# Four states in one exponential, a VectorE sum and a four-stream epilogue in the last layer of a selective-scan network

## The chip, the cores and the metric

The kernel runs on one core of one Trainium2 chip. The core has five engines with queues of their own[...]: TensorE (matmuls into PSUM), VectorE, ScalarE (activations), GpSimd (POOL in the profile) and SyncE (SP), which issues the DMA transfers. The metric is the device time of one execution in microseconds: the median of three runs.

## The reference

Four layers follow each other on x of shape (8, 48, 48, 96). Each adds to x a two-dimensional selective scan of its group-normalised input:

```
xz = gn(x) @ in_proj ;  xc, z = split(xz)            # 192 channels each
u  = silu(depthwise_conv3x3(xc) + conv_b)
for each of 4 directions k (rows, columns, and both reversed):
    dts, B, C = x_proj_k(u)                            # B and C: 16 states
    delta = softplus(dt_proj_k(dts) + bias)
    layers 0-2:  h = h * exp(delta*A) + (delta*u)*B ;  y = sum_n h*C
    layer 3:     decay = exp(cumsum(delta*A))
                 h = decay * cumsum(delta*B*u / (decay + 1e-12)) ;  y = sum_n h*C
y = sum of the directions + u * D
x = x + (layernorm(y) * silu(z)) @ out_proj
```

Layer 3 has no recurrence: its decay is a running product over the whole sequence, so with growing position exp(A * cumsum(delta)) falls until it is zero in float32, and what is added there is zero too.

## The kernel before

The eight images are taken as four pairs. For each pair the 2 x 192 channels are three tiles of 128 partitions (tile 0 and 1: the first 128 channels of each image; tile 2: the remaining 64 of both). Two phases (rows, columns) times two directions times three tiles make 12 groups for each layer and pair.

In layers 0 to 2 a group is three chunks of 768 positions with 16 states each, class `Chunk`; these units fill the first 19.6 ms. Their order within the engines is written out by hand: `keep_order` ties every instruction to the one before it on its engine. The last layer runs in a short form, class `Edge`: of each group only the 192 positions (`EDGE`) at the start of the scan are computed. The kernel checks at the end that the decay is exactly zero beyond them (`faded`, line 827) and would run the long form if it were not (lines 1199 to 1206); it doesn't here. For the short form there is no written order; the framework's scheduler orders the instructions of each engine by their place in the program and by its own estimate of when they are ready, gives out buffers, and sets all the waits.

A unit of the short form is four states (`QUAD`), handled as one tile of 128 x (4 x 192); four units make a group, and 4 x 12 x 4 = 192 units the layer. The steps of a unit, with their lines:

- `load` (857): DMA brings the four rows of C, spread over the partitions, into a "cb" tile.
- `decay` (864): ScalarE computes exp(A_n * dl) for the four states, one activation of 192 elements each, since A_n is a value per partition, passed as the activation's scale. dl is the running sum of delta (line 823), made by VectorE once for each group. The result is a "da" tile, of which there are five.
- `spread` (871, 872, 877): ScalarE makes rq = exp(-ln(da + 1e-12)), a "bb" tile of three; TensorE spreads four rows of B over the partitions into PSUM, a "b" tile of two.
- `scan` (882, 883, 885, 889, 890): VectorE multiplies b by delta*u and by rq and takes four running sums of 192; GpSimd multiplies C by da and the product by the running sums.
- `add_up` (897): TensorE adds the four products into one PSUM bank, as matmuls with the identity. At the group's end `collect` (919) adds that bank to y on VectorE.

The loop in `run` (1148 to 1184) takes one unit at a time. `get_ready` issues the decay three units ahead of the scan, and `add_up` comes four units (`LAG`) after it. Each group has a preparation (`prepare`, lines 573 to 607), which computes delta and delta*u through TensorE, ScalarE, GpSimd and VectorE, and then calls `sum_up` (823). After every unit ten steps of side work are issued (`side_step`): the epilogue of the pair before and the prologue of the pair after, whose 3 x 3 convolution is line 301.

The epilogue (926 to 1053) is a generator that goes through 16 chunks (`ECHUNKS`) of 144 positions. A chunk loads x and y (956, 958), subtracts the mean over channels by matmuls (940 to 946), squares (981), takes the mean of the squares by matmuls again, makes the scale by Ln and Exp (990, 991), multiplies (993), applies gain and offset (996), computes z by matmuls (1002, 1006), its silu (259, with a table load before and, at line 260, one after), multiplies (1015) and projects (1041 to 1043), copies (1047) and stores (1049). Its PSUM banks come from a pool of two (`bank`); its loads go one chunk ahead. The last pair's epilogue has no units beside it: line 1191 runs it to its end by itself.

Of the kernel before, what the change touches and what calls it, by code (L numbers as in the profile page):

```python
# [39 lines left out]
F32 = mybir.dt.float32  # L40
BF16 = mybir.dt.bfloat16
AF = mybir.ActivationFunctionType
ALU = mybir.AluOpType
# [6 lines left out]
P = 128  # L50
NB, H, W, DM = 8, 48, 48, 96
L = H * W
DIN = 192
NS = 16
# [8 lines left out]
EDGE = 4 * W  # L63
QUAD = 4
# [5 lines left out]
BANK = 512  # L70

SCAN = 16 * W
# [3 lines left out]
ECHUNKS = [(r * W, min(EROWS, H - r) * W) for r in range(0, H, EROWS)]  # L76
# [26 lines left out]
def ss2d_layers_kernel(ctx: ExitStack, tc: tile.TileContext, x_in, consts, weights, out):  # L103
    nc = tc.nc
# [25 lines left out]
    ident = cst[:, 0:P]  # L130
# [131 lines left out]
    def bank():  # L262
        return psum.tile([P, BANK], F32, name="ps", tag="ps")
# [353 lines left out]
    def columns_of(l, t, ph, d, n):  # L617
        k = ph + 2 * d
        return layers[l].a[:, int(t == 2), k * NS + n : k * NS + n + 1]
# [189 lines left out]
    class Edge:  # L809
# [51 lines left out]
        def decay(self, i):  # L861
            self.da[i] = da = self.quad(apool.tile([P, SCAN], F32, name="da", tag="da"))
            for j in range(QUAD):
                nc.scalar.activation(  # L864
                    da[:, j, :], self.dl, AF.Exp,
                    scale=columns_of(self.l, self.t, self.ph, self.d, QUAD * i + j),
                )

# [23 lines left out]
        def add_up(self, i):  # L892
            if i == 0:
                self.acc = pacc.tile([P, 2 * BANK], F32, name="acc", tag="acc")
            c = self.cb.pop(i)
            for j in range(QUAD):
                nc.tensor.matmul(  # L897
                    self.acc[:, :EDGE], ident, c[:, j, :],
                    start=(i == j == 0), stop=(QUAD * i + j == NS - 1),
                )  # L900
            if QUAD * i + QUAD == NS:
                late_sums.append(self.collect)
# [22 lines left out]

    def epilogue(l, p):
        ly, s = layers[l], state[l, p]
# [7 lines left out]
        def over_channels(ps, z, own, own_2, tiles):  # L935


            for t in tiles:
# [4 lines left out]
                for b in range(2):  # L943
                    o = ps[half(b), 2, :]
                    nc.tensor.matmul(o, off[:, 0:64], z[:, b, :], start=True, stop=False)  # L945
                    nc.tensor.matmul(o, own_2[:, half(b)], z[:, 2, :], start=False, stop=True)

        def three():
            return bank()[:, : 3 * EM].rearrange("p (t m) -> p t m", t=3)

        loaded = {}

        def load(i):
            at = slice(ECHUNKS[i][0], sum(ECHUNKS[i]))
            x = sm2.tile([DM, 2, EM], F32, name="ex", tag="ex")
            nc.sync.dma_start(x, src[:, :, at].rearrange("b c m -> c b m"))
            y = sm2.tile([P, 3, EM], F32, name="ey", tag="ey")
            nc.sync.dma_start(y, yd[:, :, at].rearrange("t p m -> p t m"))
            loaded[i] = x, y

        load(0)
        for _ in range(3):
            yield
        for i, (c0, m) in enumerate(ECHUNKS):
            at = slice(c0, c0 + m)
            x, y = loaded.pop(i)

# [3 lines left out]
            over_channels(ps, y, centre, centre_22, (2,))  # L971
            xn = sm1.tile([DM, 2, EM], F32, name="exn", tag="exn")
            for b in range(2):
# [4 lines left out]
            yield True  # L978
            yc = sm1.tile([P, 3, EM], F32, name="eyc", tag="eyc")
            nc.scalar.copy(yc, ps)  # L980
# [24 lines left out]
            for b in range(2):  # L1005
# [3 lines left out]
                )  # L1009
            if i + 1 < len(ECHUNKS):  # L1010
                load(i + 1)
            yield True
# [22 lines left out]
            q = m // 2  # L1035
            ps = bank()[:q, : 4 * DM].rearrange("q (h b c) -> q h b c", h=2, b=2)
            for h in range(2):
# [14 lines left out]
            yield  # L1052
        del state[l, p]


    def drain(g):
        for _ in g:
            pass
# [38 lines left out]
    def run(pairs, short):  # L1097
# [92 lines left out]
        collected()  # L1190
        drain(epilogue(*pairs[-1]))

# [109 lines left out]
```

## Time and profile before

| | us |
|---|---:|
| median of 3 runs | 21633.64 (21624.16 to 21662.88) |
| the profiled execution's own time | 21617.61 |
| its span | 21615.8 |
| layers 0 to 2, up to the first short decay (line 864) | 19594 |
| short units of the last layer, up to the last addition to y (line 919) | about 1785 |
| last epilogue to the end of the span | 237 |

| busy, share of the span | TensorE | VectorE | ScalarE | GpSimd |
|---|---:|---:|---:|---:|
| whole span | 87% | 87% | 63% | 83% |

A group of instructions in the profile is a line such as "L897 PE MATMUL acc<-cb,cst 128*128 128x192 f32 x1536 | busy us, mean ns of one | idle time of the engine just before them, and what ended it". A float32 matmul leaves two records, so the 768 matmuls of line 897 count as 1536. The "chain" follows the work back from its end: at each step to what released it, or to the instruction before it on its engine.

### The profile page before, as it was taken

The numbers are of one execution on the slowest core, as the hardware profiler recorded it, in microseconds if no ns is written. First come the engines' busy times: TensorE is split into PE (matmuls) and PEld (weight loads), VectorE is DVE, ScalarE is ACT, GpSimd is POOL, SyncE is SP. The second block draws the span as 40 slices with busy tenths as digits, with TensorE's granted clock in tenths as the row PEclk, the third lists the DMA queues.
The fourth block names the chain that finished last, engine by engine and source line by source line (L and its number), as shares of the span: only waits on it lengthen the run. The fifth ranks groups of instructions, "written<-read, shape, count | busy, mean of one in ns | idle before, by whom it ended". The sixth has DMA issues, their size and how long they took to land. (4 is left out here: it accounts for less than half of the span.)

```text
span 21615.8 us, 229908 instructions
## 1 busy us (share of the span) xinstructions
PE 18860.1 (87%) x64898; PEld 9267.7 (43%) x64898; DVE 18857.4 (87%) x15938; ACT 13615.2 (63%) x24054; POOL 18001.9 (83%) x11081
## 2 busy tenths in 40 slices
PE   8888988988988988988988988988988988988786
PEld 3333443443443444444444444444444444444555
DVE  5999999999999999999999999999999999996443
ACT  4555665665665666665666666656656655666776
POOL 5988889889898898898898888888888888895442
PEclk9999999999999999999999999999999999998887
DMA  3666666666676676676676666666666566663221
GB/s 125 187 191 190 189 193 192 188 193 190 189 200 190 189 198 189 189 199 186 189 198 190 189 194 188 187 191 190 187 191 189 187 192 186 189 191 105 74 68 52
DMA packets 1707635, 3833.01 MB, mean 177 GB/s; under 512 B 238448, under 2 KB 575216, under 8 KB 1693168
## 3 DMA queue, kind: packets, MB, share of 16 engines
q1 hardware_dynamic: 1706352, 3818.21, 60.6%
q8 instruction: 523, 8.57, 0.2%
q14 instruction: 760, 6.23, 0.1%
HBM read 3665.08 MB, written 152.27 MB: 177 GB/s over the span
## 5 line engine op out<-in xcount | busy, mean ns | idle before, releaser
L788 PE MATMUL acc<-cb,cst 128*128 128x384 f32 x27648 | 10802.0, 520 | 0.0
L754 POOL TENSOR_TENSOR cb<-cb,da 128x768 f32<-128x768 f32 x5184 | 9362.0, 1816 | 1706.4 <-DVE da L745 1047.4
L788 PEld LDWEIGHTS acc<-cb,cst 128*128 128x128 f32 x27648 | 5045.4, 197 | 3982.6 <-issue 1503.7
L745 DVE TENSOR_TENSOR_SCAN da<-da,carry,b 128x768 f32<-128x768 f32 x3456 | 6267.1, 1813 | 219.3 <-DVE b L741 1.8
L741 DVE TENSOR_TENSOR b<-du,b 128x768 f32<-128x768 f32 x5184 | 4915.6, 948 | 966.9 <-PE b L729 960.2
L712 ACT ACTIVATE da<-dl,a 128x768 f32<-128x768 f32 x5184 | 4767.5, 926 | 90.5 <-POOL cb L754 57.9
L729 PE MATMUL b<-brow,pick 48*128 48x512 bf16 (+3 forms) x10368 | 2661.3, 338 | 1629.0 <-DVE da L745 1319.0
L712 ACT ACTIVATE b<-dl,a 128x768 f32<-128x768 f32 x1728 | 1559.8, 903 | 2956.9 <-DVE da L745 2841.7
L754 POOL TENSOR_TENSOR cb<-cb,bb 128x768 f32<-128x768 f32 x1728 | 3137.3, 1816 | 230.4 <-issue 61.6
L684 POOL TENSOR_TENSOR bb<-bb,du 128x768 f32<-128x768 f32 x1728 | 3136.8, 1815 | 131.5 <-DMA bb<-xd 105.3
L745 DVE TENSOR_TENSOR_SCAN da<-da,b 128x768 f32<-128x768 f32 x1728 | 3029.9, 1753 | 109.6 <-ACT b L712 1.9
L729 PEld LDWEIGHTS <-pick 48*128 48x128 bf16 (+1 forms) x10368 | 672.9, 97 | 4467.5 <-DVE da L745 2342.7
L745 DVE TENSOR_TENSOR_SCAN bb<-b,carry,bb 128x768 f32<-128x768 f32 x1152 | 2069.5, 1796 | 21.8 <-ACT b L712 15.2
L301 PE MATMUL ps<-pad,diag 128*128 128x480 f32 (+1 forms) x4320 | 1972.1, 557 | 7.5 <-ACT u L309 5.0
L638 ACT COPY carry<-da 128x1 f32<-128x1 f32 x3456 | 627.1, 181 | 1041.1 <-DVE da L745 1026.0
L578 ACT ACTIVATE ps<-ps,w 128x384 f32<-128x384 f32 (+1 forms) x912 | 497.2, 545 | 1113.0 <-PE ps L573 1111.1
L782 PE MATMUL acc<-y,cst 128*128 128x384 f32 x1296 | 807.3, 755 | 368.0 <-ACT y L803 194.8
L301 PEld LDWEIGHTS ps<-pad,diag 128*128 128x128 f32 x4320 | 800.0, 190 | 723.9 <-issue 310.8
L591 POOL TENSOR_TENSOR lg<-lg,w 128x384 f32<-128x384 f32 (+1 forms) x912 | 894.0, 980 | 224.7 <-ACT w L589 224.7
L745 DVE TENSOR_TENSOR_SCAN bb<-b,bb 128x768 f32<-128x768 f32 x576 | 999.6, 1735 | 34.1 <-ACT b L712 28.5
L592 POOL TENSOR_TENSOR lg<-lg,e 128x384 f32<-128x384 f32 (+1 forms) x912 | 890.5, 976 | 71.2
L573 PE MATMUL ps<-dts,w 6*128 6x384 f32 (+5 forms) x2432 | 814.7, 519 | 149.3 <-DVE du L599 63.9
(141 smaller groups left out, 17513.5 us busy)
## 6 DMA issues: line engine op xcount, KB each, us to landing
cb<-xd SPq DMA_DIRECT2D x4736, 384.0 KB
cb<-xd SPq DMA_DIRECT2D x4736, 192.0 KB
bb<-xd SPq DMA_DIRECT2D x1152, 384.0 KB
bb<-xd SPq DMA_DIRECT2D x1152, 192.0 KB
yd<-y SPq DMA_DIRECT2D x48, 1152.0 KB
ey<-yd SPq DMA_DIRECT2D x256, 216.0 KB
brow<-xb SPq DMA_DIRECT2D x576, 72.0 KB
ex<-xs SPq DMA_DIRECT2D x256, 108.0 KB
```

Source lines behind the costliest of these rows:

```text
L301: nc.tensor.matmul(ps[:, :m], ly.diag[:, int(t == 2), j, :], pad[:, r0 + dy : r0 + dy + nr, dx : dx + W], start=(j == 0), stop=(j == 8),)
L573: nc.tensor.matmul(o[:, :m], ly.dtw[q0 : q0 + r, k, chans], dts[q0 : q0 + r, at], start=True, stop=True,)
L591: nc.gpsimd.tensor_sub(lg, lg, w1)
L592: nc.gpsimd.tensor_add(lg, lg, e)
L684: nc.gpsimd.tensor_mul(b, b, self.du)
L712: nc.scalar.activation(da, self.dl, AF.Exp, scale=columns_of(self.l, self.t, self.ph, self.d, n))
L729: nc.tensor.matmul(b[:, z : z + zm], w, self.brow[:k, z : z + zm], start=True, stop=True)
L741: nc.vector.tensor_mul(b, self.du, b)
L745: nc.vector.tensor_tensor_scan(way(h), way(da), way(b), start, ALU.mult, ALU.add)
L754: nc.gpsimd.tensor_mul(c, c, h)
L782: nc.tensor.matmul(self.acc[:, a, : self.m // 2], w, self.y_part(z)[:, a], start=True, stop=False,)
L788: nc.tensor.matmul(self.acc[:, a, : self.m // 2], ident, c[:, a, :], start=False, stop=(n == NS - 1),)
```

## The change

In `Edge.decay` the four scaled exponentials become one product and one exponential: GpSimd multiplies dl, read four times, with the four columns of A, each read 192 times, into the da tile, and ScalarE takes one Exp of the 768 elements in place.

In `Edge.add_up` VectorE sums the four products over the state (a `tensor_reduce` that reads the tile with the state innermost), into the first 192 columns of a further "da" tile, and one identity matmul adds that sum to the PSUM bank.

The epilogue takes a part and a number of parts. The last pair's epilogue is run as four generators, each of which takes every fourth chunk; they are stepped in turn. Streams 0 and 1 share the pool of two banks, streams 2 and 3 use the two "b" tiles of PSUM. Streams 1 to 3 keep their tiles in one "tmp" tile each and load a chunk when they begin it; stream 0 keeps the old tiles and loads its next chunk ahead. Epilogues of other pairs keep one part.

```diff
--- before.py
+++ after.py
@@ -860,11 +860,15 @@
 
         def decay(self, i):
             self.da[i] = da = self.quad(apool.tile([P, SCAN], F32, name="da", tag="da"))
-            for j in range(QUAD):
-                nc.scalar.activation(
-                    da[:, j, :], self.dl, AF.Exp,
-                    scale=columns_of(self.l, self.t, self.ph, self.d, QUAD * i + j),
-                )
+            at = (self.ph + 2 * self.d) * NS + QUAD * i
+            nc.gpsimd.tensor_mul(
+                da,
+                self.dl.unsqueeze(1).to_broadcast([P, QUAD, EDGE]),
+                layers[self.l].a[:, int(self.t == 2), at : at + QUAD].unsqueeze(2).to_broadcast(
+                    [P, QUAD, EDGE]
+                ),
+            )
+            nc.scalar.activation(da, da, AF.Exp)
 
         def spread(self, i):
             self.rq[i] = rq = self.quad(bbpool.tile([P, SCAN], F32, name="rq", tag="bb"))
@@ -892,12 +896,14 @@
         def add_up(self, i):
             if i == 0:
                 self.acc = pacc.tile([P, 2 * BANK], F32, name="acc", tag="acc")
-            c = self.cb.pop(i)
-            for j in range(QUAD):
-                nc.tensor.matmul(
-                    self.acc[:, :EDGE], ident, c[:, j, :],
-                    start=(i == j == 0), stop=(QUAD * i + j == NS - 1),
-                )
+
+            c, total = self.cb.pop(i), apool.tile([P, SCAN], F32, name="da", tag="da")[:, :EDGE]
+            nc.vector.tensor_reduce(
+                total, c.rearrange("p n m -> p m n"), mybir.AxisListType.X, ALU.add
+            )
+            nc.tensor.matmul(
+                self.acc[:, :EDGE], ident, total, start=(i == 0), stop=(QUAD * i + QUAD == NS)
+            )
             if QUAD * i + QUAD == NS:
                 late_sums.append(self.collect)
 
@@ -923,7 +929,8 @@
                 nc.sync.dma_start(s["yd"][t], y)
 
 
-    def epilogue(l, p):
+    def epilogue(l, p, part=0, parts=1):
+
         ly, s = layers[l], state[l, p]
         gn, yd, src = s["gn"], s["yd"], x_store(l, p)
         dst = x_store(l + 1, p) if l + 1 < NLAYER else None
@@ -945,38 +952,59 @@
                     nc.tensor.matmul(o, off[:, 0:64], z[:, b, :], start=True, stop=False)
                     nc.tensor.matmul(o, own_2[:, half(b)], z[:, 2, :], start=False, stop=True)
 
+        def own_bank():
+            return bank() if part < 2 else pb.tile([P, 2 * BANK], F32, name="b", tag="b")
+
         def three():
-            return bank()[:, : 3 * EM].rearrange("p (t m) -> p t m", t=3)
+            return own_bank()[:, : 3 * EM].rearrange("p (t m) -> p t m", t=3)
 
         loaded = {}
 
         def load(i):
             at = slice(ECHUNKS[i][0], sum(ECHUNKS[i]))
-            x = sm2.tile([DM, 2, EM], F32, name="ex", tag="ex")
+            if part:
+                w = tmp.tile([P, 10 * EM], F32, name="ew", tag="tmp")
+                x, xn = (
+                    w[:DM, a * EM : a * EM + 2 * EM].rearrange("p (b m) -> p b m", b=2)
+                    for a in (0, 2)
+                )
+                y, yc = (
+                    w[:, a * EM : a * EM + 3 * EM].rearrange("p (t m) -> p t m", t=3)
+                    for a in (4, 7)
+                )
+            else:
+                x = sm2.tile([DM, 2, EM], F32, name="ex", tag="ex")
+                y = sm2.tile([P, 3, EM], F32, name="ey", tag="ey")
+                xn = yc = None
             nc.sync.dma_start(x, src[:, :, at].rearrange("b c m -> c b m"))
-            y = sm2.tile([P, 3, EM], F32, name="ey", tag="ey")
             nc.sync.dma_start(y, yd[:, :, at].rearrange("t p m -> p t m"))
-            loaded[i] = x, y
-
-        load(0)
+            loaded[i] = x, y, xn, yc
+
+        mine_of = range(part, len(ECHUNKS), parts)
+        load(part)
         for _ in range(3):
             yield
-        for i, (c0, m) in enumerate(ECHUNKS):
+        for i in mine_of:
+            c0, m = ECHUNKS[i]
             at = slice(c0, c0 + m)
-            x, y = loaded.pop(i)
+            if i not in loaded:
+                load(i)
+            x, y, xn, yc = loaded.pop(i)
 
             ps = three()
             over_channels(ps, y, centre, centre_22, (0, 1))
             yield True
             over_channels(ps, y, centre, centre_22, (2,))
-            xn = sm1.tile([DM, 2, EM], F32, name="exn", tag="exn")
+            if xn is None:
+                xn = sm1.tile([DM, 2, EM], F32, name="exn", tag="exn")
             for b in range(2):
                 nc.scalar.activation(
                     xn[:, b, :], x[:, b, :], AF.Identity,
                     bias=gn[:, b, 1:2], scale=gn[:, b, 0:1],
                 )
             yield True
-            yc = sm1.tile([P, 3, EM], F32, name="eyc", tag="eyc")
+            if yc is None:
+                yc = sm1.tile([P, 3, EM], F32, name="eyc", tag="eyc")
             nc.scalar.copy(yc, ps)
             nc.scalar.activation(y, ps, AF.Square)
             yield
@@ -1007,8 +1035,8 @@
                     ps[half(b), 2, :], ly.inw[:, DIN + P : 2 * DIN], xn[:, b, :],
                     start=True, stop=True,
                 )
-            if i + 1 < len(ECHUNKS):
-                load(i + 1)
+            if not part and i + parts < len(ECHUNKS):
+                load(i + parts)
             yield True
             silu(ps, ps)
             yield True
@@ -1033,7 +1061,7 @@
                 continue
 
             q = m // 2
-            ps = bank()[:q, : 4 * DM].rearrange("q (h b c) -> q h b c", h=2, b=2)
+            ps = own_bank()[:q, : 4 * DM].rearrange("q (h b c) -> q h b c", h=2, b=2)
             for h in range(2):
                 z = slice(h * q, h * q + q)
                 for b in range(2):
@@ -1050,7 +1078,9 @@
                     out[2 * p + b, at, :].rearrange("(h q) c -> q h c", h=2), st[:, :, b, :]
                 )
             yield
-        del state[l, p]
+        state[l, p]["left"] = state[l, p].get("left", parts) - 1
+        if not state[l, p]["left"]:
+            del state[l, p]
 
 
     def drain(g):
@@ -1188,7 +1218,9 @@
             c.add_up(n)
             catch_up()
         collected()
-        drain(epilogue(*pairs[-1]))
+        streams = [epilogue(*pairs[-1], part, 4) for part in range(4)]
+        while streams:
+            streams = [g for g in streams if next(g, g) is not g]
 
     last = NLAYER - 1
     run([(l, p) for l in range(NLAYER) for p in range(NPAIR)], (last,))
```

## Prediction

> **What bounds the kernel now.** I read the page's 40 slices first, to see where the change can act at all: it edits only the short form of the last layer and the last epilogue.
>
> ```profile
> span 21615.8 us, 229908 instructions
> DVE  5999999999999999999999999999999999996443
> POOL 5988889889898898898898888888888888895442
> PEclk9999999999999999999999999999999999998887
> ```
>
> Thirty-six slices are bound by VectorE, GpSimd and TensorE together. Only the last four differ. The first short decay (line 864) starts at 19594.0 us and the last addition to y ends at 21378.8, so I cut the rest of the span in three: units with side work (the epilogue of one pair, the prologue of the next), units without, and the tail, which is the last epilogue alone.
>
> ```profile
> core 0: us, PE busy (x) PEld busy (x) DVE busy (x) ACT busy (x) POOL busy (x), PEclk, DMA share, GB/s
> 21255.00:21378.00 123.00, 72.20 (x350) 59.43 (x348) 93.79 (x164) 85.69 (x178) 84.30 (x54) 0.69 0.21 62
> 19600.00:21255.00 1655.00, 1318.82 (x7060) 916.98 (x7058) 795.67 (x1384) 1254.49 (x2307) 679.73 (x462) 0.88 0.25 72
> 21378.00:21616.00 238.00, 153.87 (x1028) 130.91 (x1026) 19.96 (x34) 118.28 (x190) 0.00 (x0) 0.73 0.13 35
> ```
>
> In 1655 us with side work TensorE is busy 80%, ScalarE 76%, VectorE 48%, GpSimd 41%. About 170 of the 192 units lie there, 9.7 us each; the last 22 or so, without side work, take 5.5 us each, and there VectorE (76%), ScalarE (70%) and GpSimd (69%) are all close. In the tail nothing is over 65%. What the units cost by line, in the window from 19600 to 21380:
>
> ```profile
> L897 PE MATMUL acc<-cb,cst 128*128 128x192 f32 x1536 | 369.5, 386 | 82.7 <-POOL cb L890 72.5 <-DVE y L919 5.4 <-POOL cb L889 3.2
> L885 DVE TENSOR_TENSOR_SCAN rq<-ones,b 128x192 f32<-128x192 f32 x768 | 363.0, 533 | 8.0 <-DVE b L883 0.5
> L890 POOL TENSOR_TENSOR cb<-cb,rq 128x768 f32<-128x768 f32 x192 | 347.7, 1812 | 415.0 <-DVE rq L885 365.7 <-ACT rq L872 25.6 <-ACT e L583 6.6
> L889 POOL TENSOR_TENSOR cb<-cb,da 128x768 f32<-128x768 f32 x192 | 347.3, 1815 | 348.4 <-ACT da L864 344.0 <-PE acc L897 4.0 <-DMA cb<-xd 0.2
> L864 ACT ACTIVATE da<-dl,a 128x192 f32<-128x192 f32 x764 | 292.2, 443 | 27.1 <-DVE dl L823 25.1 <-DVE faded L827 0.9 <-POOL cb L889 0.8
> ...
> L872 ACT ACTIVATE rq<-rq 128x768 f32<-128x768 f32 x192 | 159.2, 834 | 0.4
> ...
> L602 DVE TENSOR_TENSOR du<-ps,u 128x192 f32<-128x192 f32 x24 | 11.4, 473 | 6.0 <-ACT dl L597 6.0
> ...
> L599 DVE TENSOR_TENSOR du<-ps,u 128x192 f32<-128x192 f32 x23 | 8.0, 349 | 5.0 <-ACT dl L597 4.9
> ```
>
> GpSimd's idle time is spent on the decay and on the scans. Last, the chain of work over the same window, and the waits of the tail:
>
> ```profile
> by line: PE ps L301 15.9%; PE acc L897 10.9%; POOL cb L890 5.3%; DVE rq L885 5.0%; issue 4.9%; PE ps L940 3.1%; PE ps L941 2.6%; ACT da L864 2.5%; POOL cb L889 2.3%; DVE b L883 2.0%; ACT L259 2.0%; PE b L877 2.0%; PE ps L1042 2.0%; PE ps L9
> ```
> ```profile
> ACT eyc L980 <- PE ps L946: 50.0, 16, 22.9
> ...
> PE ps L1042 <- DVE eyc L1015: 37.9, 16, 2.4
> ACT eo L1047 <- PE ps L1043: 37.8, 16, 3.2
> ACT ps L990 <- PE ps L946: 34.5, 16, 3.6
> ```
>
> The chain's longest part (line 301) is nine blocks of convolution matmuls, 24 to 32 us each, in which TensorE serves nothing else; the change leaves them alone. In the tail ScalarE waits three times in each chunk for TensorE and TensorE waits for the rest: one chunk's chain, 14 us, run sixteen times.
>
> [...] line 872, the same shape and form as the new exponential, took 834. [...] line 602 reads u with a hop, line 599 without, (473 - 349) / 192 = 0.65 ns more. [...] In the tail the output matmuls came every 0.32 us for two records (around 21400) at a granted 0.73, and every 0.17 around 20324.
>
> **The change, part by part.**
>
> *Four exponentials become one.* ScalarE loses 768 activations, 292 us, and gains 192 like line 872, 159: 133 us less work. On the chain line 864 holds 2.5% of 1780 us, 45 us; scaled by 159/292 that leaves 24, so -20.
>
> *GpSimd multiplies instead.* 192 products of 128x768. Two inputs, both broadcast, which no row shows; nearest are lines 889 and 890, 1.815 us. Lower bound: the product costs nothing on the chain, because GpSimd is idle 59% and decays run up to three units ahead. Upper bound: the whole decay path lengthens, 1.815 + 0.834 in place of 4 x 0.373 = 1.49 (four back to back around 20315), so 1.16 us a unit, 223 us in all. I take the chain's own measure: lines 889 and 890 have 695 us of work and 7.6% of the chain, 135 us, so 0.195 us of chain for each us of work. 192 x 1.815 = 348, times 0.195: +68. Queued behind the product on GpSimd stand lines 889 and 890 of earlier units and lines 591 and 592 of the next group's delta.
>
> *VectorE adds up the four products.* A reduction of 768 elements read with a stride of 192. Lines 225 and 220 (8 and 128 elements) took 152 and 260 ns, so about 0.145 + 0.9 to 1.0 ns an element: 0.9 us without a hop penalty, 1.4 with the 0.65 ns. I take 1.4; 192 x 1.4 = 269 us. VectorE's scans and second product (lines 885, 883) have 546 us of work and 7.0% of the chain, 125 us, so 0.228: +61. Bounds: 0 and 269.
>
> *One matmul for four.* Line 897 keeps a quarter of 1536 records: 369.5 becomes 92, TensorE 277 us lighter. On the chain 10.9% of 1780 is 194 us; three quarters go: -146. What is late next: this matmul now waits for VectorE, where the reduction stands behind the scans of a unit four later, and TensorE's side matmuls stand behind it. That cost is in the upper bound of Edge below.
>
> *Buffers.* The sum takes a slot of the five "da" tiles; four decays and one sum just fit, so one spare slot goes. I cost this at nothing, covered by the three-unit lead; if the lead shrinks, it is part of the upper bound of the product.
>
> Sum for the units: -20 + 68 + 61 - 146 = -37 us.
>
> *The tail.* Now 21378.8 to 21615.8, 237 us. No work is removed: per chunk ScalarE has 118.28 / 16 = 7.4 us, TensorE 9.6 at the present clock and about 6 at the 0.17 us spacing. With four chunks in flight the busiest engine sets the time. I take ScalarE, at 85% busy, as it is in 20440 to 20480 beside other work (17.36 and 17.00 of 20 us): 139 us. Around it stay the store and load of y (21378.8 to the first matmul at 21386.4, 7.5 us), the first centring before ScalarE has work (3.5) and the end after the last copy (7). Together 157: -80 us. The streams 1 to 3 don't load ahead, so 9 loads are exposed, each about 2.9 us (21383.5 to 21386.4); while one stream waits, three others have 22 us of ScalarE work, which hides it. Without that cover, 26 us. [...] Bounds: if the clock stays at 0.73 TensorE's 153.87 us set the time, 153.87 / 0.85 + 18 = 199, -38; ScalarE at 95%, 142, -95.
>
> Total -37 - 80 = -117, from the profiled execution's 21617.6 (span 21615.8, 1.8 around it) to 21500. The median shown, 21633.6, is 16.0 above that execution; I keep this offset: 21517.
>
> **Rivals.** *Both gains stick.* ScalarE outside the convolution blocks is the engine that never rests (about 82% by the windows); relieved of 133 us, and TensorE of 277, the units shorten with it and the two added parts vanish in idle time. Units -110, tail -90: 21434. For it: VectorE and GpSimd are under half busy. Against: they are so on average only; in the stretch without side work they are at 76 and 69%, and a unit would need 3 x 1.815 = 5.4 us of GpSimd and 5.2 of VectorE in 5.5.
>
> *The units give back most of the tail's gain.* The matmul bound to VectorE and the product cost 50 us more than line 897 gave: +50 - 80 = -30, 21604, a time that can't be told from before (0.2%, 43 us, is about what a measurement of this kernel tells from no change).
>
> *Slower: GpSimd's queue sets the pace of the units.* The product stands in order behind line 890, which waits for the scans; if each decay then starts only when GpSimd is free, every unit pays the full 1.16 us, +223 - 80 = +143, and with the chain's gains of 166 not realised, 21777. It decides from 80 / 192 = 0.42 us a unit on. For it: line 890 already waits 365.7 us for the scans. Against: the product is issued three units ahead.
>
> *The streams don't overlap.* ScalarE's order could still run one chunk after another; then only the units' -37 is left: 21597. Against: no buffer is shared by more than two streams.
>
> **How the numbers follow.** Chances: the forecast 0.47, both gains 0.24, units giving it back 0.12, no overlap 0.04, slower 0.13. The forecast's own range, from the tail's bounds (-38 to -95) and +/-45 in the units, is 21450 to 21600. The range given reaches to the first rival's low side and to the point at which half of the slower case is in: 21400 to 21650. Faster: 0.47 + 0.24 and a part of the third, 0.74; within 0.2%: 0.13; slower: 0.13.
>
> **What would show it.** Line 864 x192 at about 0.83 us, a GpSimd product x192 at about 1.8, a VectorE reduction x192 at 1.4 (0.9 says no hop penalty), line 897 x384, the units' stretch shorter by 20 to 60 us, and a tail of 145 to 175 us with ScalarE over 70% busy and a granted clock above 0.8. Wrong would be: VectorE or GpSimd over 75% in the stretch with side work and a longer stretch, TensorE waiting for the reduction in the chain, or a tail over 200 us.

## The result, and the profile after

The changed kernel takes 21707.85 us (median of 12 runs, 21671.63 to 21732.28), the kernel before, run beside it, 21657.53 (12 runs, 21606.38 to 21688.58). The ratio is 1.0027, with a 95% interval of 1.0017 to 1.0037: slower by some 58 us (37 to 80), where the prediction had 117 us faster.

The profiled execution took 21728.46 us, 110.9 more than the one before. I cut it at the marks of the prediction. The units are measured from the first Ln on ScalarE (line 871 before, 875 after) to the last, which leaves out a first and a last piece that are alike: 1760 us before, 1909 after, **+149**. The tail, from the last addition to y, took 237 us before and 153.7 after, **-83**. The rest of the 111 lies ahead of the units, in code that both kernels have alike: the first Ln came 42 us later in this execution (19645.5 for 19603.9). The profiled execution of the four-stream tail alone, which shares all that code with the kernel before, has it at 19646.5 too, and over all the profiled executions of this document it lies between 19596 and 19660. So this goes with the execution and not with the change, and the windows of the units are the finer measure. How finely they repeat can be seen where two kernels share the code of the units: 1760 and 1767, 1852 and 1850.

The page's 40 slices of the changed kernel:

```profile
span 21726.7 us, 227376 instructions
...
DVE  4999999999999999999999999989999999996554
...
POOL 4998888889898898898898888888888888895553
PEclk8999999999999999999999999999999999997777
```

In the last four slices GpSimd has more to do than before and TensorE a lower clock. The windows of the changed kernel (busy us of each engine in each stretch, then the granted clock): units with side work, units without, and the tail.

```profile
core 0: us, PE busy (x) PEld busy (x) DVE busy (x) ACT busy (x) POOL busy (x), PEclk, DMA share, GB/s
19645.00:21400.00 1755.00, 1303.78 (x5955) 836.00 (x5955) 1005.61 (x1535) 1149.04 (x1789) 912.40 (x628) 0.75 0.23 66
21400.00:21573.00 173.00, 64.89 (x289) 39.39 (x287) 135.33 (x203) 87.73 (x132) 118.92 (x77) 0.57 0.20 56
21573.00:21727.00 154.00, 114.80 (x1026) 102.60 (x1026) 18.75 (x33) 110.44 (x184) 0.00 (x0) 0.87 0.20 52
```

With side work no engine is full: TensorE 74%, ScalarE 65%, VectorE 57%, GpSimd 52%. The stretch is longer all the same, and the clock in it went from 0.88 to 0.75. The tail has its clock back (0.87 for 0.73). The groups of lines over the units (busy us and mean ns of one; then the idle time ahead of them and what ended it):

```profile
L893 POOL TENSOR_TENSOR cb<-cb,da 128x768 f32<-128x768 f32 x192 | 348.3, 1822 | 94.5 <-ACT da L871 93.3 <-ACT mg L372 1.1
L894 POOL TENSOR_TENSOR cb<-cb,rq 128x768 f32<-128x768 f32 x192 | 346.9, 1810 | 325.4 <-DVE rq L889 285.5 <-ACT rq L876 7.6 <-ACT y L914 7.3
...
L901 DVE TENSOR_REDUCE da<-cb 128x192 f32<-128x768 f32 x192 | 282.1, 1488 | 22.5 <-POOL cb L893 9.4 <-PE acc L904 7.2 <-ACT rq L875 5.9
L864 POOL TENSOR_TENSOR da<-dl,a 128x768 f32<-128x768 f32 x192 | 279.5, 1468 | 71.9 <-DVE dl L823 69.7 <-PE acc L904 2.1
...
L871 ACT ACTIVATE da<-da 128x768 f32<-128x768 f32 x192 | 161.1, 839 | 116.8 <-POOL da L864 116.6
...
L904 PE MATMUL acc<-da,cst 128*128 128x192 f32 x384 | 150.2, 486 | 165.6 <-DVE da L901 154.7 <-DVE y L925 9.5 <-DMA cb<-xd 1.4
```

The product takes 1.47 us where 1.8 was predicted, the sum 1.49 where 1.4 was, the exponential 0.84 where 0.83 was. The last row is the one to look at: a quarter of the matmul records is left, but each takes 486 ns in place of 386, so that the group still costs 150 us and not 92. The chain of the changed kernel over the same window, and four of its waits (us in total, times, longest):

```profile
by line: PE ps L301 13.2%; issue 6.6%; PE ps L947 4.2%; DVE rq L889 3.7%; DVE da L901 3.7%; POOL cb L893 3.4%; PE ps L1070 3.4%; PE ps L948 3.2%; POOL da L864 3.0%; PE ps L1071 2.9%; PE ps L393 2.8%; PE ps L401 2.7%; POOL cb L894 2.4%; PE p
```

```profile
PE acc L904 <- DVE da L901: 154.7, 96, 9.6
...
PE b L881 <- DVE rq L889: 128.0, 82, 4.9
ACT da L871 <- POOL da L864: 116.6, 83, 9.1
ACT rq L875 <- POOL cb L894: 110.5, 42, 5.4
```

Line 897 held 10.9% of the chain; its successor, line 904, is not among the entries shown. In its place stand the sum (3.7%), the product (3.0%) and longer steps of the epilogue (lines 947 to 1071). TensorE waits 155 us for the sum. ScalarE now waits 110 us at line 875 until line 894 on GpSimd has let go of a "bb" tile; before, that wait was 28 us. In the tail ScalarE's waits for TensorE are down from 122 us (50.0 + 34.5 + 37.8) to 45, of which 29.7 are a single wait at the tail's start:

```profile
ACT eyc L1008 <- PE ps L953: 31.1, 4, 29.7
...
ACT ps L1018 <- PE ps L953: 13.5, 4, 3.5
```

### The profile page after: what moved, and what is told of

The parts are those of the page before. It is cut to its first block, busy times and chain, and to the rows that moved or that the text cites. A ratio compares the mean times of both kernels' runs of the same rounds, so it can differ in the third digit from the quotient of the medians.

```text
span 21726.7 us, 227376 instructions
## 1 busy us (share of the span) xinstructions
PE 18848.8 (87%) x63746; PEld 9151.5 (42%) x63746; DVE 19111.6 (88%) x16130; ACT 13503.8 (62%) x23481; POOL 18271.6 (84%) x11273
## 4 chain that ended last, share of the span: by engine, by line
PE 38%; DVE 35%; ACT 12%; issue 7%; DMA 5%; POOL 2%; SPq 1%; DVEq 0%; ACTq 0%; POOLq 0%
DVE da L745 18%; PE acc L788 16%; DVE b L741 10%; PE ps L301 5%; PE b L729 4%; PE acc L782 4%; DVE bb L745 3%; DMA cb<-xd 3%; PE ps L573 2%; ACT da L712 2%; ACT b L712 2%; ACT y L803 1%; PE ps L454 1%; DVE ps L595 1%; POOL cb L754 1%
## 5 line engine op out<-in xcount | busy, mean ns | idle before, releaser
L754 POOL TENSOR_TENSOR cb<-cb,da 128x768 f32<-128x768 f32 x5184 | 9358.6, 1815 | 1712.6 <-DVE da L745 1032.1
L745 DVE TENSOR_TENSOR_SCAN bb<-b,bb 128x768 f32<-128x768 f32 x576 | 999.6, 1735 | 34.5 <-ACT b L712 28.5
```

Of the source, the lines that this page charges most:

```text
L745: nc.vector.tensor_tensor_scan(way(h), way(da), way(b), start, ALU.mult, ALU.add)
L754: nc.gpsimd.tensor_mul(c, c, h)
```

## The experiments

All units' times and clocks below are of one profiled execution each, from first to last Ln and to about 2 us, against 1760 us and a clock of 0.87 before. Most expectations use another mark for the units, up to the last addition to y, which counts a piece more: 1771 us there is 1760 here, 1868 is 1852 (product alone), 1896 or 1897 is 1880 (sum alone), and 1929 is 1909 (the whole change). Ratios are to the kernel before, with 95% intervals that reach 0.1 to 0.2% to either side, 17 to 40 us. The expectations name their theories by letters and say what each means. Three of them come back in the text. G: the product costs through its place in GpSimd's queue. K: TensorE's work in the units keeps its clock up, and with less of it everything that passes through TensorE gets slower. X: neither; something else that moved with the edit, such as the order of the instructions.

### The three parts one at a time

The product with the one exponential alone:

```diff
-            for j in range(QUAD):
-                nc.scalar.activation(da[:, j, :], self.dl, AF.Exp, scale=...)
+            nc.gpsimd.tensor_mul(da, self.dl.unsqueeze(1).to_broadcast([P, QUAD, EDGE]), ...)
+            nc.scalar.activation(da, da, AF.Exp)
```

> The product on GpSimd with one exponential, alone; the four matmuls and the one-stream epilogue stay. Theory A (the VectorE sum is what costs: TensorE's queue stands behind it): the short units take 1771 us or less, down to about 1700, total 0 to -70 us against before. Theory B (GpSimd's queue sets the pace): the short units take about 1900 us, total about +130. Theory C (TensorE's clock falls because matmuls are gone): as A, since no matmul is gone here, granted clock in the units near 0.87.

Measured: 1.0033 (1.0020 to 1.0045); units 1852 us, +92, clock 0.83.

The sum on VectorE with one matmul alone:

```diff
-            for j in range(QUAD):
-                nc.tensor.matmul(acc, ident, c[:, j, :], ...)
+            nc.vector.tensor_reduce(total, c.rearrange("p n m -> p m n"), X, ALU.add)
+            nc.tensor.matmul(acc, ident, total, ...)
```

> The VectorE sum with one matmul, alone; four exponentials and the one-stream epilogue stay. Theory A: the short units take about 1900 us, total about +130 us, and TensorE's waits for the sum are near the 155 us of the changed kernel. Theory B: units 1735 or less, total -40. Theory C: about +130 like A, with the granted clock near 0.73.

Measured: 1.0042 (1.0028 to 1.0056); units 1880 us, +120, clock 0.74.

The four-stream tail alone:

```diff
-        drain(epilogue(*pairs[-1]))
+        streams = [epilogue(*pairs[-1], part, 4) for part in range(4)]
+        while streams:
+            streams = [g for g in streams if next(g, g) is not g]
```

> The four-stream epilogue alone. All theories: short units as before (1771 us), last epilogue 154 us in place of 237, total -83 us, ratio about 0.996. If the streams disturbed the units through the order of the program, the units would be longer than 1771.

Measured: 0.9959 (0.9945 to 0.9972); units 1767 us, tail 153 us. And the product with the tail, without the sum:

> The product on GpSimd and the four streams, without the VectorE sum. Theory A and C: total -83 to -150 us against before, ratio 0.993 to 0.996. Theory B: +130 - 83 = +50 us, ratio 1.002. If the two unit edits cost only together, it is -83 to -100 here and in the run of the sum alone nothing either.

Measured: 0.9996 (0.9988 to 1.0004); units 1850 us, tail 152 us.

So the tail is worth what was predicted, and both edits of the units cost time. Alone they cost 92 and 120 us, together 149: they overlap. None of the theories A, B and C holds alone. The product costs without the sum, against A and C, and the sum costs without the product, against B.

### What the exponential gives, and what the product takes

One Exp of dl with a fixed scale, read four times, and no product. The decays are those of a wrong A; the work left out is the product alone.

```diff
-            nc.gpsimd.tensor_mul(da, ...)
-            nc.scalar.activation(da, da, AF.Exp)
+            nc.scalar.activation(da, self.dl.unsqueeze(1).to_broadcast([P, QUAD, EDGE]), AF.Exp, scale=-1.0)
```

> As the run with the decay edit alone, with the GpSimd product left out: one Exp of dl read four times, scaled by -1 (the four states get the same decay, so the values are not the reference's). Theory P (the product on GpSimd is the cost): the units fall from 1868 us to below the 1770 of before, to about 1720, total -50 us. Theory O (the order that the scheduler makes with one exponential is worse, or the exponentials were hidden anyway): the units stay at 1800 us or more.

Measured: 1.0000 (0.9992 to 1.0009). Its window of the units (columns as above):

```profile
19636.00:21398.00 1762.00, 1383.98 (x7364) 973.42 (x7364) 863.84 (x1532) 1228.02 (x1916) 753.95 (x512) 0.86 0.26 72
```

ScalarE has 107 us less work than before (1228.02 for 1334.91) and the units are as long as before. **The relief of ScalarE is worth nothing here**, and all of the first experiment's 90 us (1852 - 1762) is the product's. Theory P had the cost right and the gain wrong: the units came back to before's time and not to 1720. The same window with the product on GpSimd, and with the product on VectorE instead:

```profile
19626.00:21478.00 1852.00, 1414.74 (x7359) 986.31 (x7356) 867.39 (x1531) 1234.66 (x1917) 1021.88 (x702) 0.83 0.23 68
```

```diff
-            nc.gpsimd.tensor_mul(da, ...)
+            nc.vector.tensor_mul(da, ...)
```

> The decay edit alone, with the product on VectorE in place of GpSimd: 192 products of about 0.95 us each. Theory G (GpSimd's queue, where the product stands among the multiplications that free the rq tiles, is what costs): the units fall from 1868 us to 1800 or less. Theory S (any further step ahead of the exponential costs): they stay above 1840 us.

```profile
19628.00:21415.00 1787.00, 1393.01 (x7368) 970.06 (x7368) 1085.12 (x1723) 1225.28 (x1910) 807.51 (x513) 0.85 0.25 70
```

Measured: 1.0004 (0.9995 to 1.0012); units 1787 us. VectorE, which has more to do than GpSimd on average, takes the product for 25 us where GpSimd takes 90. The work is much the same (1.26 us on VectorE, 1.47 on GpSimd), so it is the place that costs: on GpSimd the product stands in one queue with lines 893 and 894, the last of which hands the "bb" tiles back to ScalarE. The wait for that in the kernel with the product on GpSimd:

```profile
ACT rq L875 <- POOL cb L894: 139.8, 44, 6.4
```

It was 28.1 us before. With the product on VectorE it is still 123.7, and without any product it is 82.3 at before's time, so this wait isn't the account of the 90 us. G held for 65 of them: so much goes when the product leaves GpSimd's queue. That it goes because lines 893 and 894 then no longer stand behind a third instruction of 1.47 us is argued, not shown; the scheduler's order of the other instructions differs between these kernels too.

### What the sum takes, and what the matmuls gave

First the sum in tiles of a pool of its own, so that the "da" tiles stay as free as before:

```diff
-            total = apool.tile([P, SCAN], F32, name="da", tag="da")[:, :EDGE]
+            total = totals.tile([P, EDGE], F32, name="total", tag="total")
```

> The sum alone, written to a tile pool of its own (two of 128x192) and not to a slot of the da tiles. If the lost slot is part of the cost, the units fall from 1896 us to 1860 or less; if not, they stay within 15 us of 1896.

Measured: 1.0056 (1.0041 to 1.0071); units 1886 us against 1880 with the shared tiles. The lost slot costs nothing, as the prediction had it.

Then the matmuls are taken away and nothing is put in their place. Only the first of the four products goes into y; three are left out.

```diff
-            for j in range(QUAD):
-                nc.tensor.matmul(acc, ident, c[:, j, :], ...)
+            nc.tensor.matmul(acc, ident, c[:, 0, :], ...)
```

> As the run with the sum alone, with the VectorE sum left out: one matmul adds one state of four (three products are dropped from the output). Theory V (VectorE's reduction, and TensorE's wait for it, is the cost): the units fall from 1897 us to about 1700, as 277 us of matmul work are gone. Theory K (TensorE's clock: fewer matmuls[...]): the units stay above 1800 us with a granted clock near 0.73, though nothing waits for VectorE.

Measured: 1.0030 (1.0017 to 1.0042). Nothing waits for anything new, 576 matmuls (1152 records) are gone, and the units got **longer**:

```profile
19606.00:21430.00 1824.00, 1338.32 (x6233) 866.89 (x6232) 873.75 (x1532) 1331.84 (x2471) 753.14 (x511) 0.75 0.24 69
```

1824 us, +64, at a clock of 0.75. The next run puts TensorE's work back without the products: three float32 matmuls against a weight of zeros, of the same shape and at the same place, ahead of the one that counts. It leaves out the same three products.

```diff
+            for j in range(1, QUAD):
+                nc.tensor.matmul(acc, nothing, c[:, 0, :], ...)
             nc.tensor.matmul(acc, ident, c[:, 0, :], ...)
```

> Leaves out three products of every four, as the kernel with one matmul of one product did (its units took 1824 us at a clock of 0.75, against 1760 at 0.87 before), and adds three float32 matmuls against a weight of zeros beside that one, so that TensorE has before's number of matmuls at the same places, the earlier three without anything more to wait for than before. Theory K (TensorE's own work in the units kept its clock up; with less of it the steps of epilogue and convolutions, which pass through TensorE, got slower): units 1750 to 1785 us, clock 0.84 to 0.90, total within 0.2% of before. Theory X (it isn't TensorE's work but what else moved, the order of the instructions among it): units 1810 us or more and the total 0.25 to 0.45% over before.

Measured: 0.9994 (0.9985 to 1.0003).

```profile
19627.00:21395.00 1768.00, 1380.49 (x7366) 969.54 (x7366) 876.13 (x1530) 1335.44 (x2477) 753.49 (x511) 0.87 0.25 71
```

1768 us and a clock of 0.87: before's time is back, so the missing products themselves cost nothing. But TensorE's work is not all that came back. In the traces this kernel goes through the units in exactly the order of before, on VectorE, ScalarE, GpSimd and, the matmuls into "acc" left aside, on TensorE. In the kernel without the three matmuls 483 of ScalarE's 2477 instructions and 148 of VectorE's 1529 stand elsewhere in the order. The scheduler's order went and came back together with the work. So K fits what was measured, but X isn't ruled out: no run without the sum has the work back without the order.

What the clock does to TensorE's records can be seen in two other groups: a projection of the epilogue (line 1042 before) and an input projection of the prologue (line 393). They are the same instructions in the three kernels, and no edit touches them. Before:

```profile
L1042 PE MATMUL ps<-w,eyc 128*72 128x96 f32 x384 | 77.0, 289 | 35.5 <-DVE eyc L1015 35.4
...
L393 PE MATMUL ps<-x,w 96*128 96x480 f32 (+1 forms) x60 | 36.5, 695 | 28.4 <-ACT x L384 28.4
```

with three matmuls fewer in each unit:

```profile
L1041 PE MATMUL ps<-w,eyc 128*72 128x96 f32 x384 | 98.4, 357 | 45.0 <-DVE eyc L1014 45.0
...
L393 PE MATMUL ps<-x,w 96*128 96x480 f32 (+1 forms) x60 | 56.0, 1037 | 25.1 <-ACT x L384 24.7 <-ACT pad L397 0.4
```

and with three against zeros in their place:

```profile
L1047 PE MATMUL ps<-w,eyc 128*72 128x96 f32 x384 | 77.1, 289 | 35.1 <-DVE eyc L1020 35.1
...
L395 PE MATMUL ps<-x,w 96*128 96x480 f32 (+1 forms) x60 | 37.3, 710 | 27.5 <-ACT x L386 27.5
```

289, 357, 289 ns and 695, 1037, 710 ns. The granted clock takes two values in the records of before and of the changed kernel, 1.0 and 0.5, and each stretch at one of them, but for the last of each trace, is a whole multiple of 3.413 us (953 stretches before, 987 after). In the units the clock is at 0.5 for 26% of the time before (a mean of 0.87) and for 53% in the changed kernel (0.73); with the same two values a mean of 0.75 is half clock for half of the units. All matmuls into "ps" tiles other than the convolutions, nearly all of them side work, take 631 us before (948.9 less 317.9) and 777 with the matmuls taken away (1098.2 less 321.2); the expectations below have 621 for the first. The group itself lost 222 us, and 146 of them came back as slower matmuls elsewhere, most of them in the epilogue. The last stretch, which has no side work, took 121 us at a clock of 0.55 against 124 at 0.70 before; it is the stretches with side work that grew.

The sum with the same three matmuls against zeros:

> As the run with the sum alone, plus three matmuls with zero weights on the products that the four matmuls of before read: TensorE has the work of before again and VectorE keeps the sum. Theory V: the units get longer than 1897 us, or stay, by up to the work added. Theory K: the granted clock goes back to about 0.87 and the units get shorter than 1860 us although work is added.

Measured: 1.0046 (1.0031 to 1.0060); units 1853 us at 0.84. Against the run before it (1768), which has the same matmuls, the sum itself costs **85 us**. With the lost matmuls on both sides it costs 56 (1880 - 1824). From 1880 to 1853 the zeros seem to win 27 us, but the totals don't show it (1.0042 without them, 1.0046 with them; the profiled execution at 1880 was the slowest of its five), and by the mark of the expectation the units are at about 1870, where K had them under 1860. So here K missed in size.

### Matmuls whose result nothing reads

If TensorE's work is worth having, it might be had with any matmul. Three bfloat16 matmuls of 96 x 128 x 512 into an unused bank in each unit, with the four-stream tail:

```diff
+            for _ in range(3):
+                nc.tensor.matmul(self.acc[:, BANK:], pick2[:, 0, :], pick2[:, 0:4, :].rearrange("p n m -> p (n m)"), ...)
```

> The four-stream epilogue with the units of before, and three bf16 matmuls of 96x128 by 512 columns after each unit's add-up, which nothing reads or waits for: pure extra work for TensorE[...]. Theory K (TensorE's clock sets the length of the side work's chain): the granted clock in the units rises from 0.85 to over 0.9, the side matmuls take less than the 621 us of before, and the units are not longer than 1770 us, perhaps 20 to 60 us shorter; total at or under the 21559 of the streams alone. Theory W (TensorE's work counts as such): the units get 60 to 200 us longer.

Measured: 0.9948 (0.9935 to 0.9961), 21537.86 us, the fastest of all. The 60 to 200 us of W were the author's estimate.

```profile
19646.00:21379.00 1733.00, 1442.64 (x7923) 973.53 (x7921) 876.07 (x1530) 1339.17 (x2486) 753.55 (x511) 0.90 0.26 73
```

1733 us at a clock of 0.90, 34 us shorter than the units of the tail alone (1767) although TensorE has more to do. The intervals of the two totals overlap, though (0.9945 to 0.9972 without), so by the times alone this gain isn't shown. Six such matmuls in each unit:

> The tail in four streams, and six of the bfloat16 matmuls that nothing waits for in each unit, where three gave units of 1733 us at a clock of 0.90 and 0.9948 of before. Theory K: the clock rises further, to 0.92 to 0.95, and the units take 1690 to 1730 us: total 0.992 to 0.995. Rival (three were already enough, six only take TensorE's time, some 100 us of it more in the units): units 1740 to 1790 us, total 0.995 to 0.998.

Measured: 0.9951 (0.9933 to 0.9970); units 1738 us at 0.92. The clock rose, the time did not: three were enough. The same three beside the kernel with the matmuls taken away (three products left out), and in the whole change:

> One matmul of one product in four, no sum on VectorE (three products are dropped from the output), with three bf16 matmuls in each unit that nothing waits for. Without these it took 1824 us for the units at a clock of 0.75, against 1771 at 0.87 before. Theory K (the removed matmuls kept TensorE's clock up): the clock goes back to 0.83 or more, the side matmuls from 777 us towards 650, and the units fall to 1700 to 1775 us; total at or under before. Theory X (something else in the shortened add-up delays the units): the units stay at 1810 us or more.

> The whole change with the same three free matmuls in each unit. Theory K: the clock in the units rises from 0.73 to 0.85 or more and the units fall from 1929 us to about 1850, total below the 21708 of the change by 50 us or more. Theory W: the units get longer than 1929 us.

Both went against K; X and W came out. Measured: 1.0045 (1.0031 to 1.0058), units 1854 us at 0.79; and 1.0036 (1.0024 to 1.0048), units 1931 us at 0.76. The clock was still low with these fillers (0.79, against 0.87 with zeros); their records take 207 us in the units (0.36 us each), those of the zeros 291. But the matmuls into "ps" tiles did get faster (1053 us for 1098) and the units got no shorter for it, so the clock alone doesn't set their time. Nor were the fillers free of all waiting: they write into the second bank of the tile that is added to y, and VectorE's addition waited 60.9 us where it waited 54.0 without them, in the whole change 108.6 for 75.9. And the order of the instructions differs here as well. Which of these it was isn't shown.

With the product on VectorE, the tail and the fillers together:

> One exponential for four states with its product on VectorE, the tail in four streams, three matmuls that nothing waits for in each unit; the matmuls of the products stay four. The three apart gave: units 1787 against 1760 us (product on VectorE), a tail 80 us shorter (streams), units 27 us shorter (fillers). If they add up: units about 1760 us, total 0.9955 to 0.997. If ScalarE's 106 us of relief are worth something once the clock is up: units under 1733 us and total under 0.9948. If VectorE's 280 us more are worse with the clock up: units over 1790 us, total over 0.997.

Measured: 0.9982 (0.9973 to 0.9991); units 1815 us at 0.87. The last of the three cases: with the fillers, too, the exponential's relief has no worth, and the product on VectorE costs 82 us against the filled tail (1733).

### The whole change with TensorE's work put back

> The whole change, and beside its one matmul three float32 matmuls against a weight of zeros, so that TensorE has before's number of matmuls. The units took 1909 us at a clock of 0.73 without them, 1760 at 0.87 before. If the lost work of TensorE is a third part of the 149 us, beside product and sum: units 1845 to 1885 us at 0.80 to 0.87, total 1.000 to 1.002 of before. If product and sum together account for them, and the low clock only follows from their waits: units 1890 to 1930 us, total 1.0025 to 1.005.

```diff
+            for j in range(1, QUAD):
+                nc.tensor.matmul(acc, nothing, c[:, j, :], ...)
             nc.tensor.matmul(acc, ident, total, ...)
```

Measured: 1.0031 (1.0022 to 1.0041).

```profile
19637.00:21548.00 1911.00, 1494.61 (x7343) 1041.74 (x7343) 1121.14 (x1716) 1232.42 (x1916) 1027.04 (x701) 0.81 0.23 66
```

1911 us against 1909: the clock is at 0.81 for 0.73, and nothing is gained. So with TensorE's matmuls as many as before, product and sum alone make the 151 us, and taking the matmuls away is then worth 2. The matmuls into "ps" tiles did get faster (1055 us for 1118). Whether that is worth nothing here, or whether the added work takes what the higher clock gives, this run can't tell.

## Why the prediction was wrong

The units of the runs that the account rests on:

| in the units | units, us | clock |
|---|---:|---:|
| before: four exponentials, four matmuls | 1760 | 0.87 |
| one exponential, no product | 1762 | 0.86 |
| one exponential, product on VectorE | 1787 | 0.85 |
| one exponential, product on GpSimd | 1852 | 0.83 |
| one matmul, no sum | 1824 | 0.75 |
| one matmul and three against zeros, no sum | 1768 | 0.87 |
| sum, one matmul and three against zeros | 1853 | 0.84 |
| sum, one matmul | 1880 | 0.74 |
| the whole change | 1909 | 0.73 |
| the whole change and three against zeros | 1911 | 0.81 |

**The step that failed is "One matmul for four": -146.** It scaled a group's share of the chain by the work that is taken from the group. Measured on its own the removal gave +64; within the whole change, beside product and sum, it gave -2 (1909 for 1911). The same way of reckoning failed in "Four exponentials become one": -20 predicted, +2 measured. A share of the chain says where the last wait happened to end. Take the work away, and the chain can run through what stood beside it: with the units of before cut into eighths, TensorE is 65 to 86% busy in one and ScalarE 71 to 82%, so that none sets the pace alone. That both shares gave nothing is shown; this reason for it is argued. The removal on its own also went with something that the sum of the prediction doesn't have, a lower clock (0.75 for 0.87). The prediction had the clock in view for the tail (a mean of 0.73; where it found two records of the output matmuls every 0.32 us the granted clock was 0.50, where every 0.17 it was 1.00) and didn't ask the same of the units, from which it took 277 us of TensorE's work. That the clock would rise in the tail (0.87 measured) was its estimate; what sets the clock is not shown by these runs. How much of the +64 is the clock's and how much belongs to the other order stays open.

**The added terms were right in kind and too small.** "GpSimd multiplies instead": +68 predicted, +90 measured, although the instruction took 1.47 us in place of 1.815. "VectorE adds up the four products": +61 predicted, +85 measured (56 with the matmuls gone), with 1.49 us in place of 1.4. The estimate with the 0.65 ns an element by which line 602 was slower than line 599 (473 and 349 ns for 192 elements) is the one that came near, 0.9 us without it is far off; no run here sums without a hop. The prices per us of work were too low: 90 us for 282 us of products is 0.32 and not 0.195, 85 for 286 us of sums is 0.30 and not 0.228. Both together, with TensorE's matmuls as many as before, cost 151 and not 175. So the units gained nothing from the matmuls where 146 was booked and nothing from the exponential where 20 was, and paid 151 where 129 was. With its two gains left out, the prediction's own sum is +129 in the units and, with the tail's -80, +49 in all; the runs gave +58 (37 to 80). That it comes so near is partly luck: each added term was larger alone, and together they overlap.

One reading of the chain was off, without effect on the sum: the nine blocks of convolution take 36 to 37 us each, and 24 to 32 are the chain's pieces of them.

**"The tail" was right**: -80 predicted, -83 measured, 153.7 us against 157, ScalarE busy 72%, clock 0.87. **"Buffers"** at nothing was right: 1886 against 1880 us.

**The rivals.** "GpSimd's queue sets the pace of the units" had the right side and the nearest time, 21777 against 21708. Its price was 1.16 us a unit; the product alone costs 90 / 192 = 0.47, just past its threshold of 0.42, and the whole change 149 / 192 = 0.78. Its 21777 holds nothing for the sum, so that its nearness is partly luck too. "Both gains stick" fell with the run without the product and the run without the sum. "The units give back most of the tail's gain" named the wait of the matmul for the sum, which is there (155 us), and put the give-back at 50 us of 80; it was more than all. "The streams don't overlap" fell with the tail.

**The signs it named.** Counts, tail and durations came out as listed, but for the product's (1.47 us for 1.8); the units' stretch did not. As the sign of failure it named VectorE or GpSimd over 75% busy with side work; they were at 57 and 52%. TensorE waiting for the sum, the other sign, was there.

What stays open: how product and sum come to overlap, why the fillers that went with 34 us less beside four matmuls did nothing beside one, and above all whether the removal of the matmuls cost time through the clock or through the order in which the framework's scheduler then puts the instructions. The run without the product has a different order on VectorE and ScalarE and takes before's time, so a different order does not by itself cost time. But the one run in which the totals show that added matmuls brought the time back has before's order again to the last instruction; the sum and the whole change got their matmuls back without it, and there the totals show no gain (1.0046 for 1.0042, 1.0031 for 1.0027). A run with before's order and fewer matmuls would decide it.

## What to carry to other kernels

A group's share of the chain is no estimate of what its removal gives (here -146 and -20 booked, +64 and +2 measured): where several engines are 70 to 80% busy and wait for each other in turn, take such a gain as nothing until an engine is shown to be full, and book added work on the queues at its price (here 0.32 and 0.30 us for each us of work). Before work is taken off TensorE, look at its clock in that stretch: here the matmuls that stayed took 146 us more at the lower clock (0.75 for 0.87), which ate most of the 222 us that went, whatever lowered it. And where a scheduler orders the instructions, compare the order of two kernels before a difference is put down to the work. A serial stretch on idle engines is the safer place: the four streams there gave 83 us where the arithmetic promised 80.

## What the runs showed of the hardware

- Taking three of four identity matmuls from each unit, 222 us less in that group (361 to 139), went with a granted clock of 0.75 for 0.87, and the kernel was 0.3% slower. The same number of matmuls against zeros brought clock (0.87) and time (0.9994) back, and the old order of the instructions with them. In the whole change the same zeros raised the clock from 0.73 to 0.81 and left the units at 1911 us for 1909.
- GpSimd's product of two broadcast operands, 128 x 768 in float32, took 1.47 us; with both operands read in full (lines 893 and 894) it took 1.81 to 1.82.
- VectorE's float32 product of the same two broadcast operands took 1.26 us. In that kernel GpSimd's products of lines 893 and 894 took 1.96 and 1.92 us, 0.14 and 0.11 more than before.
- `tensor_reduce` over four elements at a stride of 192 took 1.49 us for 768 elements, and GpSimd's products kept their 1.81 to 1.82 us beside it.
